# Attention block with a causal convolution: output products of ten groups of four blocks as seven products instead of eight

## The chip, the cores and the metric

The kernel runs on one core of a Trainium2 chip. The metric is the device time of one execution in microseconds (us). Before the change it is 2947.87 us, the median of 3 runs (2943.88 to 2949.68).

## The reference

Four sequences of 1024 tokens with 1024 features, f32 throughout. A conditioned attention layer is added to x, and then a causal convolution over tokens with four taps (the taps are the rows of `cond`):

```
scale, shift = split(emb @ W_emb + b_emb)
xn = rms_norm(x, g_norm) * (1 + scale) + shift
q, k, v = split(xn @ W_qkv)                  # 16 heads of 64
q, k = rms_norm(q, g_q), rms_norm(k, g_k)
attn = softmax(q @ k.T / 8)
o = attn @ v
x = x + (o + o @ W_out)                      # o @ (W_out + I)
x = x + causal_conv1d(x, cond) + b           # K = 4, per feature
```

## The kernel before

Work goes by *units*: one sequence b, one pair of heads c, one half of the queries. There are 64, 16 for each sequence. A unit takes the scores of its two heads against the keys in eight steps (`Unit.scores`, matrix products in line 626, copied out of PSUM in line 634), the running maximum on VectorE (643), the maximum over partitions on GpSimd (648), the shift on VectorE (662), exp on ScalarE (666), the sum on GpSimd (668), and in the next unit the product with v (689) and the sum over keys (709). `divide` (749) writes o of the pair, transposed, and it is stored in DRAM (`scrO`).

Between these steps lie *pieces* of other work, which `between(p)` lists for unit p in seven slots. A projection piece (586) is one of seven products of the qkv projection of a later pair of pairs: that projection already works with seven products for eight, on sums of its inputs (`Chunk.combine`, `scrA`) and of its weights (`Weights.combine`, `scrB`). An output piece (`Out`) takes one block of 128 features by 512 tokens of one sequence: transposes of x into PSUM (805), eight matrix products with a column block of W_out, into whose diagonal block the identity was added (799, 819), a copy to SBUF (837), the last tap on ScalarE (839), three taps on VectorE (851), transposes (862), and the store. From unit 16 on each unit has one output of the sequence before (`plan`); in the last 16 units the numbers are 1, 0, 1, 0, 1, 0, 1, 1, 0, 1, 0, 1, 3, 3, 3, 0 (`last_plan`). The outputs of the last sequence follow at the end. o comes back from DRAM in `gather`, one tile of 256 KB for each block of features in eight buffers (tag `ob`). Weight blocks use the same buffers in the first units.

The order on TensorE, VectorE, ScalarE and GpSimd is the order in which the Python program emits instructions. A planned clock (`tick`, `clock`) decides when deferred steps are emitted: `defer` after a time, `defer_quiet` not while the shifts and exps run (`loud`), `defer_gap` in the time in which VectorE would wait for the maximum over partitions (`fill_gap`, once in a unit), and `need` at once. `split` puts the last 25 us of a unit's pieces (`BEHIND`) behind its last scores, beside the softmax. All transfers are issued on SP, which works through them in an order of the scheduler's own; a transfer that waits holds those behind it.

## Time and profile before

| what | value |
|---|---|
| median of 3 runs | 2947.87 us |
| the profiled execution, its span | 2953.38 us, 2951.6 us |
| TensorE, VectorE, ScalarE, GpSimd busy | 96%, 75%, 57%, 48% |
| granted TensorE clock, mean | 0.988 |
| bytes moved, mean rate | 411.89 MB, 140 GB/s |

The profile is one execution. A matrix product in f32 appears as two records. A group's busy time is the union of its instructions, its mean is that of one. "Idle before" is the time for which the engine stood still ahead of the group's instructions, with what ended it.

### The profile page before, as it was taken

To read this page: it belongs to the slowest core of one execution; us is meant where nothing else is said; L and a number is where in the kernel's file an instruction comes from. 1 tells how busy PE (TensorE), PEld (TensorE's weight loads), DVE (VectorE), ACT (ScalarE), POOL (GpSimd) and SP (SyncE) were. 2 spreads that over 40 slices of the span, in tenths; PEclk is the share of its full clock that TensorE was granted. 3 is DMA by queue.
4 is the path that set the end of the run, shared out by engine and by line. 5 is a ranking of instruction groups with operands and counts; after the bars stand their busy time and mean duration, and the time that the engine had idled before them with its cause. 6 is when DMAs were issued, how large, how long until landed. Compare 5 with 4: busy or idle time off the path is not lost.

```text
span 2951.6 us, 32110 instructions
## 1 busy us (share of the span) xinstructions
PE 2830.6 (96%) x10601; PEld 1336.0 (45%) x10601; DVE 2228.2 (75%) x2563; ACT 1694.3 (57%) x2233; POOL 1402.3 (48%) x574
## 2 busy tenths in 40 slices
PE   7989988999999999999999999999999999999898
PEld 3544434444444444444444444444444444444344
DVE  3578878888877777787877777878777877787863
ACT  3155757765656666665555666665565656565432
POOL 2045555556645544545544553545555555553420
PEclk9999999999999999999999999999999999999999
DMA  7764445643333454543533354553343333323333
GB/s 275 254 214 149 148 162 165 197 132 111 115 111 112 146 168 156 177 132 104 157 118 93 126 164 150 177 159 107 100 154 109 103 115 100 111 79 111 108 96 114
DMA packets 401085, 411.89 MB, mean 140 GB/s; under 512 B 40544, under 2 KB 331672, under 8 KB 400920
## 3 DMA queue, kind: packets, MB, share of 16 engines
q1 hardware_dynamic: 400920, 409.84, 43.9%
q8 instruction: 85, 1.39, 0.2%
q14 instruction: 80, 0.66, 0.1%
HBM read 334.26 MB, written 75.48 MB: 139 GB/s over the span
## 4 chain that ended last, share of the span: by engine, by line
PE 75%; DVE 9%; ACT 7%; POOL 3%; issue 2%; DMA 2%; SPq 1%; DVEq 0%; ACTq 0%; POOLq 0%
PE pqkv_P L586 29%; PE po L819 14%; PE pav L689 14%; PE s L626 13%; ACT sp L634 3%; DVE mx L643 2%; POOL sum L668 2%; DVE sp L662 2%; ACT sp L666 2%; DVE y L851 1%; POOL mb L648 1%; PE tot L709 1%; PE qkt L457 1%; PE otp L862 1%; PE po L805 1%
## 5 line engine op out<-in xcount | busy, mean ns | idle before, releaser
L586 PE MATMUL pqkv_P<-w_P,a 128*128 128x384 f32 x3504 | 1189.9, 492 | 27.5 <-issue 11.3
L668 POOL TENSOR_TENSOR sum<-sum,sp 128x1024 f32<-128x1024 f32 x384 | 974.9, 2539 | 58.9 <-ACT sp L666 32.4
L586 PEld LDWEIGHTS pqkv_P<-w_P,a 128*128 128x128 f32 x3504 | 650.7, 191 | 493.2 <-issue 73.2
L634 ACT COPY sp<-s 128x1024 f32<-128x1024 f32 x512 | 511.1, 1015 | 461.7 <-PE s L626 363.9
L643 DVE TENSOR_TENSOR mx<-mx,sp 128x1024 f32<-128x1024 f32 x384 | 524.5, 1366 | 223.0 <-ACT sp L634 199.1
L662 DVE TENSOR_TENSOR sp<-sp,mbp 128x1024 f32<-128x1024 f32 x512 | 604.6, 1212 | 34.3 <-ACT mbp L657 34.2
L648 POOL PARTITION_ALL_REDUCE mb<-mx x64 | 223.9, 3499 | 837.6 <-DVE mx L643 513.5
L666 ACT ACTIVATE sp<-sp 128x1024 f32<-128x1024 f32 x512 | 526.6, 1055 | 117.1 <-DVE sp L662 113.3
L626 PE MATMUL s<-qT,kT 64*128 64x512 f32 x2048 | 520.3, 624 | 40.6 <-ACT sp L634 24.9
L689 PE MATMUL pav<-sp,v 128*64 128x512 f32 x2048 | 472.5, 604 | 0.0
L819 PE MATMUL po<-ob,wo 128*128 128x512 f32 x992 | 441.0, 597 | 2.5 <-DMA ob<-scrO 1.6
L851 DVE SCALAR_TENSOR_TENSOR y<-x,cols,y 128x512 f32<-128x512 f32 x192 | 324.2, 1689 | 109.0 <-ACT y L839 104.4
L668 POOL TENSOR_TENSOR sum<-sp,sp 128x1024 f32<-128x1024 f32 x64 | 151.3, 2363 | 476.3 <-ACT sp L666 293.1
L626 PEld LDWEIGHTS s<-qT,kT 64*128 64x128 f32 x2048 | 171.3, 186 | 333.4 <-issue 167.8
L689 PEld LDWEIGHTS pav<-sp,v 128*64 128x64 f32 x2048 | 136.8, 138 | 321.8 <-issue 309.9
L819 PEld LDWEIGHTS po<-ob,wo 128*128 128x128 f32 x992 | 184.6, 192 | 212.9 <-issue 204.1
L643 DVE TENSOR_TENSOR mx<-sp,sp 128x1024 f32<-128x1024 f32 x64 | 126.9, 1983 | 86.3 <-ACT sp L634 85.5
L837 ACT COPY x<-po 128x512 f32<-128x512 f32 x64 | 37.5, 586 | 228.3 <-PE po L819 211.9
L605 DVE TENSOR_TENSOR qk<-u,pqkv_P 128x256 f32<-128x256 f32 x256 | 105.5, 412 | 60.7 <-PE pqkv_P L586 58.7
L657 ACT COPY mbp<-mb 128x1024 f32<-128x1024 f32 x64 | 65.1, 1017 | 123.7 <-POOL mb L648 123.6
L449 DVE TENSOR_TENSOR qk<-qk,ms 128x1024 f32<-128x1024 f32 x64 | 123.0, 1922 | 2.2
L435 ACT ACTIVATE sq<-qk 128x512 f32<-128x512 f32 x128 | 76.0, 626 | 55.4 <-DVE qk L605 55.4
(84 smaller groups left out, 1659.5 us busy)
## 6 DMA issues: line engine op xcount, KB each, us to landing
a<-scrA SPq DMA_DIRECT2D x215, 512.0 KB
w_P<-scrB SPq DMA_DIRECT2D x64, 768.0 KB
w_P<-in_L_cond_W_qkv_dram SPq DMA_DIRECT2D x144, 256.0 KB
wo<-in_L_cond_W_out_dram SPq DMA_DIRECT2D x128, 256.0 KB
scrA<-r SPq DMA_DIRECT2D x26, 896.0 KB
xc<-in_x_dram SPq DMA_DIRECT2D x64, 256.0 KB
out_dram<-ot SPq DMA_DIRECT2D x64, 256.0 KB
rec<-scrR SPq DMA_DIRECT2D x124, 128.0 KB
```

What stands on the lines that cost most here:

```text
L449: nc.vector.tensor_mul(qk, qk, self.ms[g].unsqueeze(2).to_broadcast([P, 4 * HT, D]))
L586: nc.tensor.matmul(pm, (chunks[0, k].r(place) if a is None else a[:, k, :])[:, t % 2 * P : (t % 2 + 1) * P], w[:, k, :], start=(k == 0), s ...
L626: nc.tensor.matmul(ps[:, h, :], pr.kT[kt // HT][h * D : (h + 1) * D, kt % HT * P : (kt % HT + 1) * P], pr.qT[self.half][h * D : (h + 1) * ...
L634: nc.scalar.copy(sp, ps)
L643: nc.vector.tensor_max(self.mx, self.mx if kt > 1 else self.sp[0], self.sp[kt])
L648: nc.gpsimd.partition_all_reduce(self.mb.rearrange("p h q -> p (h q)"), self.mx.rearrange("p h q -> p (h q)"), P, bass_isa.ReduceOp.max,)
L662: nc.vector.tensor_sub(self.sp[kt], self.sp[kt], self.mb)
L666: nc.scalar.activation(sp, sp, AF.Exp)
L668: nc.gpsimd.tensor_tensor(self.sum, self.sum if kt > 1 else self.sp[0], sp, ALU.add)
L689: nc.tensor.matmul(self.pav[h * D : (h + 1) * D, :], self.pr.v[kt // HT][:, kt % HT, h * D : (h + 1) * D], self.sp[kt][:, h, :], start=(kt ...
L819: nc.tensor.matmul(self.pm, self.w[kh][:, k % KH, :], oTs[b, k, half], start=False, stop=(k == NJ - 1),)
L851: nc.vector.scalar_tensor_tensor(self.y, self.x1[:, k : k + HN], cols[:, r : r + 1], self.y, ALU.mult, ALU.add)
```

## The change

For sequences 0 and 1 and for half of the outputs of sequence 2, four outputs (features j and j + 4, both halves of the tokens) are made together in a `Quad`, of seven products with four matrix products each. The input is halves of o and four sums of them (`OutSums`, made once for each sequence and stored in `scrS`), the weight quarters of W_out + I and four differences of them (`OutWeights`, made in units 8 to 14 and stored in `scrW`). A sum of products is kept in two SBUF tiles (`u2`, `u4`) and added on VectorE. The products start in unit 18, seven in four units, later seven in five. The other eight outputs of sequence 2 are whole products in units 60 to 62, and those of sequence 3 follow as before. Tiles of tag `ob` are now two of 1 MB instead of eight of 256 KB, for weights, sums and o; input tiles of the projection (tag `a`) are three instead of four. The diagonal add moves from GpSimd to VectorE for the remaining whole outputs, and the halo copy from VectorE to ScalarE. `x1` has two buffers, the taps of sequence 2 are always deferred out of the loud time, which ends 4 us later, and outputs are stored once they are 30 us old. The sum over keys of the last two units takes four products of 32 rows each instead of two of 64.

```diff
-        for e in list(idle):
+        for e in sorted(idle, key=lambda e: e[2][2][0] != "qk"):
...
             d, k = self.d, self.k
             self.b = {}
+            four = apool.tile([P, 4, HN], F32, tag="ob", name=f"b_{self.name}", bufs=2)
             for kh in range(2):
                 for y in range(2):
-                    t = apool.tile([P, HN], F32, tag="ob", name=f"b_{self.name}_{kh}_{y}", bufs=8)
+                    t = four[:, 2 * kh + y, :]
                     self.b[kh, y] = t[:, :W3]
...
-            return apool.tile([P, KH, QN], F32, tag="a", name=name, bufs=4)
+            return apool.tile([P, KH, QN], F32, tag="a", name=name, bufs=3)
...
-            loud[1] = loud[0] + NT * step + 1.0
+            loud[1] = loud[0] + NT * step + LOUD
...
-            oT = apool.tile([P, HN], F32, tag="oT", name=f"oT_{self.name}", bufs=3)
+            oT = apool.tile([P, HN], F32, tag="oT", name=f"oT_{self.name}", bufs=2)
...
+            nc.sync.dma_start(scrO[b][self.half][:, c, :], oT)
+    scrO = [
+        [dram.tile([P, NJ, HN], F32, tag=f"o_{b}_{h}", name=f"scrO_{b}_{h}") for h in range(2)] for b in range(B)
+    ]
     def gather(b, half):
-        for k in range(NJ):
-            if (b, k) == (B - 1, NJ - 1):
-                continue
-            need("oT", b, k, half)
-            if (b, half) == (B - 1, 1):
-                if k % 2 == 0:
-                    pair = apool.tile([P, KH, QN], F32, tag="a", name=f"ob_{b}_{k}_{half}", bufs=4)
-                    pair = pair.rearrange("p k t -> p (k t)")
-                ob = pair[:, k % 2 * HN : (k % 2 + 1) * HN]
+        for kh in range(2):
+            n = KH - kh if b == B - 1 else KH
+            for k in range(n):
+                need("oT", b, kh * KH + k, half)
+            if half and b == B - 1:
+                four = apool.tile([P, 8, QN], F32, tag="r", name=f"ob_{b}_{kh}_{half}", bufs=2)
+                four = four.rearrange("p i t -> p (i t)").rearrange("p (k t) -> p k t", t=HN)
             else:
-                ob = apool.tile([P, HN], F32, tag="ob", name=f"ob_{b}_{k}_{half}", bufs=8)
-            nc.sync.dma_start(ob, scrO[b, k, half])
-            oTs[b, k, half] = ob
+                four = apool.tile([P, KH, HN], F32, tag="ob", name=f"ob_{b}_{kh}_{half}", bufs=2)
+            nc.sync.dma_start(four[:, :n, :], scrO[b][half][:, kh * KH : kh * KH + n, :])
+            for k in range(n):
+                oTs[b, kh * KH + k, half] = four[:, k, :]
+    OUT = ("P1", "P2", "P6", "P5", "P3", "P7", "P4")
+    scrW = dram.tile([P, 7, KH, HN], F32, tag="W", name="scrW")
+    OUT_W = {"P5": 0, "P7": 1, "P4": 2, "P6": 3, "P1": 4, "P2": 5, "P3": 6}
+    scrS = [dram.tile([P, 4, KH, HN], F32, tag=f"S_{b}", name=f"scrS_{b}") for b in range(B - 1)]
+    OUT_S = {"P6": 0, "P3": 1, "P7": 2, "P5": 3}
+    class OutWeights:
+        def __init__(self, k):
+            self.k = k
+        def load(self):
+            k = self.k
+            self.b = apool.tile([P, 4, HN], F32, tag="ob", name=f"W_{k}", bufs=2)
+            for kh in range(2):
+                src = w_out[(kh * KH + k) * P : (kh * KH + k + 1) * P, :]
+                nc.sync.dma_start(self.b[:, 2 * kh : 2 * kh + 2, :], src.rearrange("p (y d) -> p y d", y=2))
+            defer_gap(5.0, ("W", k), 0.6, self.diagonals)
+        def diagonals(self):
+            k = self.k
+            for i in (0, 3):
+                d = self.b[:, i, k * P : (k + 1) * P]
+                nc.vector.tensor_tensor(d, d, ident, ALU.add)
+            for i, name in ((0, "P1"), (2, "P2"), (3, "P3")):
+                nc.sync.dma_start(scrW[:, OUT_W[name], k, :], self.b[:, i, :])
+            defer_gap(5.0, ("W", k), 2.8, self.combine)
+        def combine(self):
+            b11, b12, b21, b22 = (self.b[:, i, :] for i in range(4))
+            for dst, p0, p1 in ((b11, b12, b11), (b12, b22, b12), (b22, b22, b11), (b21, b21, b22)):
+                nc.vector.tensor_tensor(dst, p0, p1, ALU.subtract)
+            nc.sync.dma_start(scrW[:, :4, self.k, :], self.b)
+    class OutSums:
+        def __init__(self, b, k):
+            self.b, self.k = b, k
+        def load(self):
+            b, k = self.b, self.k
+            self.o = apool.tile([P, 4, HN], F32, tag="ob", name=f"S_{b}_{k}", bufs=2)
+            for h in range(2):
+                for kh in range(2):
+                    need("oT", b, kh * KH + k, h)
+                    nc.sync.dma_start(self.o[:, 2 * h + kh, :], scrO[b][h][:, kh * KH + k, :])
+            defer_gap(5.0, ("S", b, k), 2.8, self.combine)
+        def combine(self):
+            o11, o12, o21, o22 = (self.o[:, i, :] for i in range(4))
+            for dst, p0, p1, op in (
+                (o22, o21, o22, ALU.add),
+                (o21, o11, o21, ALU.subtract),
+                (o11, o22, o11, ALU.subtract),
+                (o12, o12, o11, ALU.subtract),
+            ):
+                nc.vector.tensor_tensor(dst, p0, p1, op)
+            nc.sync.dma_start(scrS[self.b][:, :, self.k, :], self.o)
+    class Quad:
+        def __init__(self, b, j):
+            self.b, self.j = b, j
+            self.outs = {
+                name: Out(b, c, half) for name, c, half in (("P2", j, 0), ("P3", j + KH, 0), ("P7", j + KH, 1), ("P4", j, 1))
+            }
+            self.o, self.w = {}, {}
+        def load(self, name):
+            b, j = self.b, self.j
+            if name in self.outs:
+                self.outs[name].load_x()
+            o = self.o[name] = apool.tile([P, KH, HN], F32, tag="ob", name=f"o_{b}_{j}_{name}", bufs=2)
+            if name in OUT_S:
+                for k in range(KH):
+                    need("S", b, k)
+                src = scrS[b][:, OUT_S[name], :, :]
+            else:
+                half, kh = {"P1": (0, 0), "P2": (0, 1), "P4": (1, 1)}[name]
+                for k in range(kh * KH, (kh + 1) * KH):
+                    need("oT", b, k, half)
+                src = scrO[b][half][:, kh * KH : (kh + 1) * KH, :]
+            nc.sync.dma_start(o, src)
+            for k in range(KH):
+                need("W", k)
+            w = self.w[name] = wpool.tile([P, KH, P], F32, tag="wo", name=f"wq_{b}_{j}_{name}", bufs=3)
+            nc.sync.dma_start(w, scrW[:, OUT_W[name], :, j * P : (j + 1) * P])
+        def product(self, name):
+            b, j = self.b, self.j
+            out = self.outs.get(name)
+            if name == "P7":
+                out.residual(whole=True)
+                nc.vector.tensor_add(self.u4, self.u4, out.pm)
+            if name in ("P2", "P3", "P4"):
+                out.residual()
+                pm = out.pm
+            else:
+                pm = ps_m.tile([P, 512], F32, tag="m", name=f"po_{b}_{j}_{name}")
+            for k in range(KH):
+                nc.tensor.matmul(
+                    pm,
+                    self.w[name][:, k, :],
+                    self.o[name][:, k, :],
+                    start=(k == 0 and name not in ("P2", "P3", "P4")),
+                    stop=(k == KH - 1),
+                )
+            tick(3.5)
+            if name == "P1":
+                self.u2 = apool.tile([P, HN], F32, tag="ou2", name=f"ou2_{b}_{j}", bufs=1)
+                nc.scalar.copy(self.u2, pm)
+            elif name == "P5":
+                self.u4 = apool.tile([P, HN], F32, tag="ou4", name=f"ou4_{b}_{j}", bufs=1)
+                nc.vector.tensor_add(self.u4, self.u2, pm)
+            elif out:
+                out.open()
+                nc.vector.tensor_add(out.x1[:, PAD:], self.u4 if name in ("P3", "P7") else self.u2, pm)
+                out.last_tap(out.x1[:, PAD:])
+            if name in ("P6", "P7"):
+                nc.vector.tensor_add(self.u2, self.u2, pm)
...
-            defer(4.5 if j < KH or b >= B - 2 else 8.0, ("wo", self.name), self.diagonal)
+            defer(4.5, ("wo", self.name), self.diagonal)
         def diagonal(self):
             d = self.w[self.j // KH][:, self.j % KH, :]
-            (nc.vector if self.b == B - 1 or self.b == B - 2 and self.half else nc.gpsimd).tensor_tensor(d, d, ident, ALU.add)
-        def residual(self):
+            nc.vector.tensor_tensor(d, d, ident, ALU.add)
+        def residual(self, whole=False):
...
-            if taken:
-                need("y", taken.pop())
+            self.open()
+            nc.scalar.copy(self.x1[:, PAD:], self.pm)
+            self.last_tap(self.pm)
+        def open(self):
+            if len(taken) == 2:
+                need("y", taken.pop(0))
             taken.append(self.name)
-            x1 = apool.tile([P, PAD + HN], F32, tag="x1", name=f"x1_{self.name}", bufs=1)
-            self.x1 = x1
-            if half:
-                nc.vector.tensor_copy(x1[:, :PAD], halo[:, j, :])
-            else:
-                nc.vector.memset(x1[:, :PAD], 0.0)
-            nc.scalar.copy(x1[:, PAD:], self.pm)
+            x1 = self.x1 = apool.tile([P, PAD + HN], F32, tag="x1", name=f"x1_{self.name}", bufs=2)
+            nc.scalar.copy(x1[:, :PAD], halo[:, self.j, :] if self.half else none)
+        def last_tap(self, src):
+            j = self.j
             self.y = apool.tile([P, HN], F32, tag="x", name=f"y_{self.name}", bufs=6)
             nc.scalar.activation(
                 self.y,
-                self.pm,
+                src,
                 AF.Identity,
                 bias=cols[:, R_CB + j : R_CB + j + 1],
                 scale=tap_self[:, j : j + 1],
             )
-            (defer if self.b >= B - 2 and self.half else defer_quiet)(2.0, ("y", self.name), self.taps)
+            (defer if self.b == B - 1 else defer_quiet)(2.0, ("y", self.name), self.taps)
...
-    BEHIND = 25
+    BEHIND = 26
...
+    AGE = 30.0
+    LOUD = 5.0
+    AGE_REST = 5.0
+    W_AT = 3
+    outs, norms, chunks, weights, doubles, quads = {}, {}, {}, {}, {}, {}
+    LAST = (B - 1) * 2 * NJ
+            if n in (PB - 1, PB) and i % 14 == W_AT:
+                free(lambda: OutWeights((n - PB + 1) * 2 + i // 14).load())
+    def out_next(m):
+        at = REST.index(m) + 1 if m in REST else 0
+        out_load(m + 1 if m not in REST else REST[at] if at < len(REST) else LAST)
...
-    plan = [1] * NB
-    last_plan = [1, 0, 1, 0, 1, 0, 1, 1, 0, 1, 0, 1, 3, 3, 3, 0]
-    assert sum(plan) == NB and sum(last_plan) == NB and len(plan) == NB
+    NQ = 2 * KH + KH // 2
+    NG = NQ * len(OUT)
+    def products_until(p):
+        q = p - NB - 2
+        return min(max(q * 7 // 4 if q < 2 * NB else 56 + (q - 2 * NB) * 7 // 5, 0), NG)
+    REST = [(B - 2) * NB + h * NJ + j for h in range(2) for j in (2, 3, 6, 7)]
+    REST_PLAN = {p: n for p, n in zip(range(B * NB - 4, B * NB - 1), (3, 3, 2))}
+    def out_load_product(g):
+        b, i = divmod(g, 4 * len(OUT))
+        j, i = divmod(i, len(OUT))
+        if g < NG:
+            if i == 0:
+                quads[b, j] = Quad(b, j)
+            quads[b, j].load(OUT[i])
+    def out_product(g):
+        b, i = divmod(g, 4 * len(OUT))
+        j, i = divmod(i, len(OUT))
+        def step():
+            if g == 0:
+                out_load_product(0)
+            quad = quads[b, j]
+            quad.product(OUT[i])
+            if OUT[i] in quad.outs:
+                late.append((clock[0], quad.outs[OUT[i]].store))
+            out_load_product(g + 1)
+        pieces = [(3.95 if OUT[i] in ("P2", "P3", "P7", "P4") else 3.5, step)]
+        return [(0.0, lambda: store(AGE))] + pieces
...
-        pl = last_plan if b == B - 1 else plan
-        slots[0].append((0.45, store))
-        ks = range(sum(pl[:i]), sum(pl[: i + 1])) if b else ()
-        if b and i == 0:
-            slots[0] += [(0.0, lambda: gather(b - 1, 0)), (0.0, lambda: out_load((b - 1) * NB))]
-        for a, k in enumerate(ks):
-            m = (b - 1) * NB + k
-            at = 4 if len(ks) == 1 else 2 * a + 1
-            slots[at] += out_pieces(m)
-            if a:
-                slots[at].append((0.45, store))
-            if k == NJ - 1:
-                slots[at].append((0.0, lambda: gather(b - 1, 1)))
-            slots[at].append((0.0, lambda m=m: late.append(outs[m].store)))
+        slots[0].append((0.0, lambda: store(AGE)))
+        d, k = divmod(p - 11, NB)
+        if 0 <= d < B - 1 and k % 2 == 0 and k < NJ:
+            slots[0].append((0.0, lambda: OutSums(d, k // 2).load()))
+        for a, g in enumerate(range(products_until(p), products_until(p + 1))):
+            slots[(2, 5)[a]] += out_product(g)
+        if p in REST_PLAN:
+            at = sum(n for q, n in REST_PLAN.items() if q < p)
+            for m in REST[at : at + REST_PLAN[p]]:
+                if m in REST[:: len(REST) // 2]:
+                    slots[6].append((0.0, lambda m=m: gather(B - 2, m // NJ % 2)))
+                slots[6] += [(0.0, lambda: store(AGE_REST))] + out_pieces(m)
+                slots[6].append((0.0, lambda m=m: late.append((clock[0], outs[m].store))))
```

## The prediction

> **What bounds the kernel now.** I read the page's engine table and groups first, then TensorE's timeline for one unit, then the stretches by stage, and the chain last.
>
> ```profile
> PE 2830.6 (96%) x10601; PEld 1336.0 (45%) x10601; DVE 2228.2 (75%) x2563; ACT 1694.3 (57%) x2233; POOL 1402.3 (48%) x574
> ...
> L819 PE MATMUL po<-ob,wo 128*128 128x512 f32 x992 | 441.0, 597 | 2.5 <-DMA ob<-scrO 1.6
> ```
>
> TensorE is busy 96% of the span, but modelled ends make that figure soft. The timeline of one unit of the second batch is harder evidence:
>
> ```profile
> 1009.76 7.03 PE L819 MATMUL po<-ob,wo 128*128 128x512 f32 x16
> 1016.63 5.32 PE L586 MATMUL pqkv_P<-w_P,a 128*128 128x384 f32 x16
> 1021.88 1.99 PE L626 MATMUL s<-qT,kT 64*128 64x512 f32 x8
> ...
> 1029.62 2.04 PE L626 MATMUL s<-qT,kT 64*128 64x512 f32 x8 [0.25 <-ACT sp L634]
> 1031.60 3.65 PE L689 MATMUL pav<-sp,v 128*64 128x512 f32 x16
> ```
>
> Each row starts where the last ends; the only wait is 0.25 us. So in this stage what TensorE has to do is the time. The chain shows what removing such work is worth. It lists every whole output product as one piece:
>
> ```profile
> 1009.92 6.87 PE po L819 x16
> ...
> 1052.15 6.88 PE po L819 x16
> ...
> 2196.49 6.87 PE po L819 x16
> ...
> 2275.13 6.87 PE po L819 x16
> ...
> 2354.06 6.87 PE po L819 x16
> ...
> 2432.70 6.87 PE po L819 x16
> ```
>
> One output's 8 matrix products (16 records, two passes each for f32) take 6.87 us, so 0.859 us per product. With an output in each unit the units are 42.2 to 42.7 us apart. At the end of the table the plan has an output in every second unit: 78.64, 78.93, 78.64 us for two units, against 2 x 42.67 = 85.3. Leaving out one output gave back 6.6 us. Its TensorE work is 6.87 plus 0.44 (residual transposes) plus 0.59 (output transposes) = 7.9. So 84% of removed TensorE time comes back; the rest turns into small waits.
>
> The other engines' room, by stretches (us, then busy PE, PEld, DVE, ACT, POOL, clock, DMA share, GB/s):
>
> ```profile
> 165.00:783.00 618.00, 574.95 (x2226) 267.37 (x2225) 505.90 (x579) 400.00 (x516) 342.13 (x128) 0.98 0.48 154
> ...
> 1009.00:1051.60 42.60, 42.35 (x159) 19.90 (x158) 31.37 (x32) 23.81 (x34) 22.02 (x10) 1.00 0.41 131
> 1263.00:1306.00 43.00, 42.32 (x168) 19.82 (x166) 38.25 (x45) 29.22 (x37) 22.38 (x9) 1.00 0.47 144
> ```
>
> VectorE is at 74% in a plain unit, 89% in a unit that also prepares the next batch, 82% in the first batch, where TensorE idles 43 of 618 us. VectorE is the engine to watch.
>
> **What it removes.** Ten groups of four outputs go from 4 x 8 = 32 products to 7 x 4 = 28; 24 outputs stay whole. 512 becomes 280 + 192 = 472. 40 x 0.859 = 34.4 us of TensorE time, all in stages where TensorE sets the pace. Residual and output transposes stay as many. Times 0.84 (the ratio above): 28.9 us come back. That ratio includes the smaller cover that every wait has behind a shorter unit.
>
> Moved: outputs begin in unit 18 rather than 16, and the last three full units get 3, 3 and 2 whole outputs rather than 3, 3 and 3. Each matrix product is still done once, where TensorE is the bound at both places, so 0.
>
> **What it adds on VectorE.** Rows of the tiles y and oT (shortest, median, longest in ns), and a group kept apart by shape:
>
> ```profile
> L851 DVE SCALAR_TENSOR_TENSOR y<-x,cols,y x192: 741/1515/2900, 803.7 to 2945.6; 128x512 f32<-128x512 f32 x192
> ...
> L749 DVE TENSOR_TENSOR oT<-pav,rec x64: 676/682/692, 220.5 to 2876.7; 128x512 f32<-128x512 f32 x64
> ...
> L507 DVE TENSOR_TENSOR b<-b,b 128x384 f32<-128x384 f32 x48 | 33.7, 701 | 8.7 <-DMA b<-in_L_cond_W_qkv_dram 7.6
> ```
>
> - A group of seven products has 8 adds with one operand in PSUM (P2, P6, P5, P3, P4 one each, P7 three). The nearest row is L749, 0.68 us, steady. 80 x 0.68 = 54.4. Against it, 32 halo copies (24.7 us in the groups) and 32 memsets (2.0) go over to ScalarE: net +28 us over 42 units, 0.7 per unit.
> - 12 sums of o with 4 adds each, both operands in SBUF: by L507 scaled from 384 to 512 elements 0.93 us, so 3.7 per set, 44.9 in all. Weights: 4 x (4 x 0.93 + 2 x 0.42, the VectorE row of the diagonal add) = 18.2.
> - Here a rule speaks against the change. L851, with two SBUF inputs, takes from 0.74 to 2.9 us; L749, reading PSUM, never over 0.69. The Trainium skill (SBUF — State Buffer, "SBUF: two separate sides") says that a VectorE operation with two SBUF inputs and a GpSimd operation reading SBUF take an exclusive lock on one port pair, so one waits for the whole of the other. By it each of the 64 SBUF adds could wait one GpSimd add (2.54 us): 64 x 2.54 = 163 us of VectorE time more. By the row, which holds such waits already in its mean, 63 in all. I take the row: these adds are released in the gap in which VectorE waits for the maximum over partitions. The 40 diagonal adds that leave GpSimd (0.94 each) help a little.
>
> Sum on VectorE: 28 + 44.9 + 18.2 = +91 us, 2319 of some 2930, 79% against 75%. In a plain unit it lies in 11 us of idle: 0. If that cover went, 1.8 us in each of 42 units, 76 us. In the first batch 33 us of it falls into ten units, with 7 us idle in each: between 0 and 15, I take 2. ScalarE: 30 fewer copies of 0.586 and 64 tiny ones of 0.2: -5 us. It now waits for VectorE's add before it takes the last tap; that wait lies beside TensorE: 0.
>
> **What it adds in waits.** Tiles of o come as 1 MB in two buffers. Product g+1's tile loads from the end of product g-1, normally some 38 us ahead. But a set of sums occupies one of the two from its load to its store. While it does, the next tile can start only when the last product ends, and by the order of instructions three projections stand between (3 x 2.58 + 0.44 = 8.2 us; in the other case 9.1). Eight of the twelve sets fall so. What 1 MB takes is not in the trace. The chain shows smaller loads:
>
> ```profile
> 124.73 6.33 DMA a<-scrA
> ...
> 137.41 5.16 DMA a<-scrA
> ...
> 2674.84 4.89 DMA ob<-scrO
> ```
>
> 256 KB took 4.89 us, 512 KB 5.2 to 6.3; so 0.3 to 1.4 per 256 KB, and 1 MB some 5.8 to 9.1, estimated. The Trainium skill (DMA: Bandwidth & Descriptors, "Anatomy of one DMA — SWDGE (gpsimd) path") fits 2.0 us plus bytes by 436 GB/s, which would be 4.4 us and no wait; it is for another queue than SP's, and already the 256 KB row exceeds it. By the rows the wait is 0 to 1.5, plus what holds SP up; 0.5 x 8 = 4 us, bounds 0 and 24.
>
> - Projection inputs have three buffers, not four. SP then waits for the pair of projections just before, and has two pairs (10.3 us) for a load of 5 to 6. Queued behind on SP: the small transfers of the row sums and the next w and o. 215 loads; TensorE waited for one, 0.4 us. I take 0, bounds 0 and 20.
> - SP issues 84 more transfers, some 0.4 us each, 34 us over the whole span. Bytes: +70 (o) +24 (sums) +11 (W) -8 -20 +17.5 = +95 MB on 412, so 140 GB/s becomes 175; the first 50 us ran at 306. 0.
> - Whole outputs at the end gather 1 MB at a change of half where 256 KB pieces could follow each other: 2.5 us late, in a unit of 46 us with 7 idle. 0, bounds -6 (the unit with two outputs) and 5.
> - Start: weight tiles are freed four at a time. SP's loads begin up to 2.7 us later (the next stores are at 54 to 58, not 53). 1 us, bounds -2 and 6.
>
> **Sum.** -28.9 + 2 + 4 + 1 = -21.9. Against its own execution: span 2951.6 (2953.4 with what lies around) to 2929.7 (2931.5). That execution is 5.5 above the median of the runs, 2947.9; from the median, **2926**.
>
> **Rivals.**
> - *VectorE becomes the bound in part* (0.22). For: 89% in preparing units, 82% in the first batch, and adds that may wait for GpSimd. Against: the gap before the shifts. In full it costs 1 us in each of 8 preparing units, 15 in the first batch where I took 2, and 1 us for each pinned tile where I took 0.5: 8 + 13 + 4 = 25 more, which would leave no gain. At half of that, 12.5: **2938**.
> - *Slower* (0.10): SP's queue comes late. With three buffers each load of projection inputs waits at SP's head for a TensorE event one pair later, and what stands behind comes late in turn. For: SP already waits there 103 us in 66 cases. Against: TensorE waited 0.4 us. Price: 215 loads, one in four 1 us late is 54; with 21.9 off, **2980**. It decides from 22 us, 0.1 us per load.
> - *Nothing changes* (0.06): the waits equal the gain: **2948**.
> - *The ratio is 1, not 0.84, and no load is late* (part of the likeliest): -34.4, **2913**.
>
> **How the numbers follow.** The forecast holds with 0.62, range 2912 to 2933. VectorE 0.22, nothing 0.06, slower 0.10. About 0.2% (6 us) is what a measurement can tell. Faster 0.84 (the first two), within 0.06, slower 0.10. The range runs from 2909 (ratio 1 and 4 us from the shorter last unit) to 2950, past the second rival and the third, leaving most of the slower one out.
>
> **What would show it.** Right: output products 472, some 3.44 us per group of four; units with two of them 42 us apart, with one 38; no PE wait for o over 2 us. VectorE near 2320 us. Wrong: PE idle before the output or projection products on DMA (pinned tile, three buffers); PE waiting for ScalarE's score copies (VectorE late); a first batch longer than 618 us by over 5; a GpSimd idle time before the maximum that grows.

## The result and the profile after

On one chip, against the kernel before, the change gives 2915.59 us (median of 6 runs, 2911.43 to 2922.92) against 2945.89 (6 runs, 2943.3 to 2949.68). The ratio is 0.9899, with an interval of 0.9882 to 0.9915: faster by 1.0%. The forecast was 2926 with 2909 to 2950. The profiled spans are 2951.6 before and 2917.7 after, so 33.9 us went (30.3 by the medians) where the sum had 21.9. That is close to the 34.4 us of the products, but not by the way the sum describes: several of its small terms are wrong in size or sign, others are missing, and they nearly cancel.

The engine line of the page after, and the groups that answer to those shown of before (busy us, mean ns of one, idle before):

```profile
PE 2797.4 (96%) x10529; PEld 1322.4 (45%) x10529; DVE 2183.2 (75%) x2652; ACT 1692.7 (58%) x2269; POOL 1347.7 (46%) x534
...
L986 DVE SCALAR_TENSOR_TENSOR y<-x,cols,y 128x512 f32<-128x512 f32 x192 | 249.4, 1303 | 61.2 <-ACT y L974 56.6
...
L950 PE MATMUL po<-ob,wo 128*128 128x512 f32 x352 | 159.6, 606 | 4.4 <-DMA ob<-scrO 4.4
L881 PE MATMUL po_P<-o_P,wq_P 128*128 128x512 f32 x320 | 144.0, 592 | 0.2 <-DVE u L610 0.2
...
L881 PE MATMUL po<-o_P,wq_P 128*128 128x512 f32 x240 | 108.0, 592 | 0.0
```

The output products are now 352 + 320 + 240 records here and 32 in the last block's own group (from the tile `oT`): 944, two each, so 472 as counted. The seven products (L881) waited for no transfer at all. VectorE's busy time did not rise by 91 us, it fell by 45. The three taps (L986) alone fell by 75; their group of before was:

```profile
L851 DVE SCALAR_TENSOR_TENSOR y<-x,cols,y 128x512 f32<-128x512 f32 x192 | 324.2, 1689 | 109.0 <-ACT y L839 104.4
```

TensorE's timeline of one unit with two products:

```profile
1252.91 3.60 PE L881 MATMUL po<-o_P,wq_P 128*128 128x512 f32 x8
1256.35 5.32 PE L589 MATMUL pqkv_P<-w_P,a 128*128 128x384 f32 x16
...
1264.53 3.60 PE L881 MATMUL po_P<-o_P,wq_P 128*128 128x512 f32 x8
...
1278.87 2.04 PE L629 MATMUL s<-qT,kT 64*128 64x512 f32 x8 [0.31 <-ACT sp L637]
```

As before, the rows follow each other and the one wait is 0.31 us. The chain has the product as a piece of 3.43 to 3.44 us, half of the 6.87 of a whole output:

```profile
1253.08 3.44 PE po L881 x8
...
1264.69 3.43 PE po_P L881 x8
```

The same stretches of time as before, which hold almost the same units (us, then busy PE, PEld, DVE, ACT, POOL, clock, DMA share, GB/s):

```profile
165.00:783.00 618.00, 576.75 (x2219) 266.84 (x2220) 511.14 (x602) 399.26 (x512) 339.38 (x129) 0.98 0.53 171
1009.00:1051.60 42.60, 42.35 (x168) 19.33 (x166) 32.57 (x40) 24.94 (x35) 19.63 (x9) 1.00 0.54 180
1263.00:1306.00 43.00, 42.69 (x163) 20.24 (x162) 34.55 (x39) 26.79 (x34) 20.67 (x8) 1.00 0.54 174
```

TensorE fills a unit as before. What VectorE lost and gained shows in its groups, kept apart by shape:

```profile
L747 DVE TENSOR_TENSOR oT<-pav,rec 128x512 f32<-128x512 f32 x64 | 44.0, 688 | 42.5 <-DMA rec<-scrR 39.5 <-issue 2.9
...
L835 DVE TENSOR_TENSOR S<-S 128x512 f32<-128x512 f32 x48 | 33.0, 688 | 1.2
...
L809 DVE TENSOR_TENSOR W<-W 128x512 f32<-128x512 f32 x16 | 14.0, 875 | 0.4
...
L900 DVE TENSOR_TENSOR ou<-ou,po_P 128x512 f32<-128x512 f32 x20 | 13.7, 684 | 13.9 <-PE po_P L881 13.9
```

One row is new in kind: ahead of `oT`, the product with the reciprocal of the row sums, VectorE now stands idle 39.5 us for the transfer of the reciprocals, in 18 waits. Before it was 4.9 us in 4:

```profile
DVE oT L749 <- DMA rec<-scrR: 4.9, 4, 2.0
```

Only 7.3 us of these waits lie between units 8 and 16, where they will turn out to cost time (experiment 4).

**Where the 33.9 us went.** A mark that both traces have is the start of each unit's sum over keys on TensorE (L709 before, L707 after). The mark of unit u, counted from 0, lies in unit u + 1; "units 8 to 16" is the time from mark 8 to mark 16, and "units 1 to 8" that from the first mark to mark 8. The table takes the difference of the times between two marks, beside the difference in TensorE work between them, from the records there: a product at 0.859 us, the transposes of a residual at 0.44 and of an output at 0.59.

| stretch between marks | before, us | after, us | difference | TensorE work | rest |
|---|---|---|---|---|---|
| to the first mark | 200.4 | 193.5 | -6.9 | 0 | -6.9 |
| units 1 to 8 | 316.4 | 307.7 | -8.6 | 0 | -8.6 |
| units 8 to 16 | 304.5 | 315.4 | +10.9 | -7.3 | +18.2 |
| units 16 to 48 | 1401.0 | 1361.5 | -39.5 | -37.0 | -2.5 |
| units 48 to 59 | 439.2 | 450.3 | +11.0 | +17.3 | -6.2 |
| units 59 to 63 | 210.8 | 210.3 | -0.5 | -7.3 | +6.8 |
| to the end | 79.3 | 79.0 | -0.3 | 0 | -0.3 |
| all | 2951.6 | 2917.7 | -33.9 | -34.4 | +0.5 |

Rounding leaves 0.1 here and there. The "rest" is not nothing everywhere: it is two gains ahead of unit 8, a loss of 18.2 in units 8 to 16, small gains in the middle and a loss in the tail. A second profile of the changed kernel (span 2916.8) has its marks within 1.6 us of the first from unit 16 on, but 4.1 us earlier at unit 8; so the split between the second and the third row is good to some 4 us, their sum to 1. Early gains also shrink again: the five kernels without the products (the kernel before and experiments 6 to 9) reach mark 8 between 508.8 and 516.7 us, but mark 16 between 818.0 and 822.1. So part of the 18.2 can be the loss of what was gained ahead of it.

### The profile page after: what moved, and what is told of

It is laid out like the page before. It is cut to its first block, busy times and chain, and to the rows that moved or that the text cites. A ratio compares the mean times of both kernels' runs of the same rounds, so it can differ in the third digit from the quotient of the medians.

```text
span 2917.7 us, 32188 instructions
## 1 busy us (share of the span) xinstructions
PE 2797.4 (96%) x10529; PEld 1322.4 (45%) x10529; DVE 2183.2 (75%) x2652; ACT 1692.7 (58%) x2269; POOL 1347.7 (46%) x534
## 3 DMA queue, kind: packets, MB, share of 16 engines
q8 instruction: 84, 1.38, 0.2%
## 4 chain that ended last, share of the span: by engine, by line
PE 71%; DVE 13%; ACT 7%; DMA 4%; issue 3%; POOL 1%; SPq 1%; DVEq 0%; ACTq 0%; POOLq 0%
PE pqkv_P L589 28%; PE pav L692 14%; PE s L629 13%; PE po L950 5%; DVE mx L646 4%; PE po_P L881 4%; PE po L881 3%; ACT sp L637 3%; DVE sp L665 2%; ACT sp L669 1%; PE qkt L459 1%; DVE y L986 1%; PE tot L707 1%; DMA rec<-scrR 1%; PE otp L997 1%
## 5 line engine op out<-in xcount | busy, mean ns | idle before, releaser
L671 POOL TENSOR_TENSOR sum<-sum,sp 128x1024 f32<-128x1024 f32 x384 | 958.1, 2495 | 73.2 <-ACT sp L669 43.1
L646 DVE TENSOR_TENSOR mx<-mx,sp 128x1024 f32<-128x1024 f32 x384 | 514.6, 1340 | 166.2 <-ACT sp L637 137.8
L986 DVE SCALAR_TENSOR_TENSOR y<-x,cols,y 128x512 f32<-128x512 f32 x192 | 249.4, 1303 | 61.2 <-ACT y L974 56.6
L646 DVE TENSOR_TENSOR mx<-sp,sp 128x1024 f32<-128x1024 f32 x64 | 107.8, 1685 | 103.7 <-ACT sp L637 103.7
L950 PE MATMUL po<-ob,wo 128*128 128x512 f32 x352 | 159.6, 606 | 4.4 <-DMA ob<-scrO 4.4
L881 PE MATMUL po_P<-o_P,wq_P 128*128 128x512 f32 x320 | 144.0, 592 | 0.2 <-DVE u L610 0.2
L881 PE MATMUL po<-o_P,wq_P 128*128 128x512 f32 x240 | 108.0, 592 | 0.0
```

What stands on the lines that cost most here:

```text
L646: nc.vector.tensor_max(self.mx, self.mx if kt > 1 else self.sp[0], self.sp[kt])
L671: nc.gpsimd.tensor_tensor(self.sum, self.sum if kt > 1 else self.sp[0], sp, ALU.add)
L881: nc.tensor.matmul(pm, self.w[name][:, k, :], self.o[name][:, k, :], start=(k == 0 and name not in ("P2", "P3", "P4")), stop=(k == KH - 1),)
L950: nc.tensor.matmul(self.pm, self.w[kh][:, k % KH, :], oTs[b, k, half], start=False, stop=(k == NJ - 1),)
L986: nc.vector.scalar_tensor_tensor(self.y, self.x1[:, k : k + HN], cols[:, r : r + 1], self.y, ALU.mult, ALU.add)
```

## The experiments

Each was timed beside the kernel before on the same chip. Diffs are against the changed kernel unless another is named.

**1. The eighth product back** (P1 made twice in one accumulation).

```diff
-            for k in range(KH):
+            times = 2 if name == "P1" else 1
+            for a in range(times):
+                for k in range(KH):
...
-                    start=(k == 0 and name not in ("P2", "P3", "P4")),
-                    stop=(k == KH - 1),
+                        start=(a == 0 and k == 0 and name not in ("P2", "P3", "P4")),
+                        stop=(a == times - 1 and k == KH - 1),
```

> The changed kernel, in which the product P1 of each of the ten groups is accumulated twice (so its outputs are not the reference's): 40 matrix products more, no other work, no other data. It prices the TensorE time that the change takes away. Theory: in these units TensorE's own work is the time, and 3.44 us per group come back in full: +34 us against the changed kernel, so level with the kernel before or up to 4 us above. The step of the prediction (0.84 of it comes back): +29. Rival: the gain comes from something else (shorter waits, cheaper taps), and the products lie partly beside waits: +15 or less.

2948.0 us (13 runs), ratio 0.9987 (0.9979 to 0.9996), span 2948.1. The marks move away from the changed kernel's by 3.2 us per group, from +2.8 at unit 16 to +34.8 at unit 58: 32.0 of 34.4, so 93% in this profile, where the forecast had 84%. Each of the ten groups costs 2.6 to 3.4 us in the one unit that its product lies in. The whole is less sure: the spans of the two profiles differ by 30.4 us, since the tail of this one is some 4 us shorter, and the timed ratios by 0.0088, 26 us, with an interval of some 6 either way. So the units' lengths speak for 93%; the timed runs do not tell it from 84%. All the rest of the change together is worth little: with 32 products' time per group again, the kernel is 0.13% from the one before.

**2. The sums of o and the differences of the weights left out** (loads, stores and transfers stay).

```diff
-            for dst, p0, p1 in ((b11, b12, b11), (b12, b22, b12), (b22, b22, b11), (b21, b21, b22)):
-                nc.vector.tensor_tensor(dst, p0, p1, ALU.subtract)
...
-                nc.vector.tensor_tensor(dst, p0, p1, op)
```

> The changed kernel without the 64 adds on VectorE that make the sums of o and the differences of the weights (loads and stores stay, the outputs are not the reference's). Some 47 us of VectorE time go. Theory: what units 8 to 16 lose (19 us like for like) comes from the late transfers of the row sums, of which these adds hold up a part, since the reciprocal stands behind them on VectorE: -5 us. Rival, VectorE is the bound in the first batch: -15 or more. Rival, SP's queue alone: 0 within 3.

2903.3 us (4 runs), ratio 0.9838 (0.9824 to 0.9851), span 2899.1, so 18.6 less than the changed kernel. That is the size of the rival, VectorE as the bound, and not of the theory; experiments 4 and 5 decide on the cause. The two groups are busy 47 us in all, but the time does not come back where most of them stand: the marks part by 12.7 us between units 8 and 16, by 1.5 up to 20, and by 0.5 from there to 58, although 8 of the 12 sets of sums lie there. So some 30 of these adds (16 of weights, 12 to 16 of o) cost 13 us in the first batch, while the later ones are nearly free. And without them VectorE's wait for the reciprocals falls to a third, between units 8 and 16 from 7.3 us to nothing, although every transfer is still there:

```profile
DVE oT L747 <- DMA rec<-scrR: 13.3, 9, 2.7
```

**3. The loud time as before** (taps may stand beside the shifts and exps again).

```diff
-    LOUD = 5.0
+    LOUD = 1.0
```

> The changed kernel with LOUD back at 1.0, so that the taps on VectorE are deferred 4 us less and run again beside the sums on GpSimd. Theory: the taps become dearer (mean 1.30 us back toward 1.69, VectorE +60 us or more), but VectorE is not the bound, so the time is within 5 us of the changed kernel. Rival, cheaper taps are a part of the gain: +10 us or more.

2924.43 us (4 runs), ratio 0.9908 (0.9895 to 0.9922), span 2923.3. The group of the taps:

```profile
L986 DVE SCALAR_TENSOR_TENSOR y<-x,cols,y 128x512 f32<-128x512 f32 x192 | 300.4, 1569 | 65.7 <-ACT y L974 61.2
```

1569 ns against 1303: the same work at another place takes 51 us more of VectorE. Its price in time is small, +5.6 us in this profile, which it has at unit 48 and keeps to the end; by the ratios 0.0009, which is inside the intervals. VectorE's busy time and the kernel's time are two things.

**4. The division 3 us later on the planned clock.** The row sums go to DRAM, come back as a small tile, are inverted on VectorE, go out and come back as `rec`; then VectorE multiplies.

```diff
-    DIVIDE = 18.0
+    DIVIDE = 21.0
```

> The changed kernel with DIVIDE 21 in place of 18: the division of o is emitted 3 us later on VectorE. Theory: VectorE stands 39.5 us in 18 waits for the transfer of the reciprocals, with shifts behind it that free the PSUM of the scores; 3 us later most of these waits are gone (under 12 us), and the time falls by 4 to 10 us, most of it in units 8 to 17. Rival, these waits lie beside other work: 0 within 3. Rival, the PSUM of the value product comes free too late: +5 or more.

2904.81 us (5 runs), ratio 0.9842 (0.9828 to 0.9855), span 2903.9, 13.8 less (17 by the ratios); expected were 4 to 10. VectorE's waits for `rec` are all but gone:

```profile
DVE oT L747 <- DMA rec<-scrR: 3.0, 3, 1.7
```

Between units 8 and 16 it is 306.7 us long instead of 315.4, near the 302.7 of the kernel without the adds. The granted clock of this stretch says the same. Two rows, the changed kernel and this one:

```profile
501.19:816.63 315.44, 292.98 (x1135) 135.43 (x1133) 258.79 (x314) 197.63 (x247) 169.03 (x64) 0.98 0.53 173
```

```profile
502.86:809.54 306.68, 287.82 (x1135) 134.64 (x1133) 261.77 (x313) 197.26 (x247) 171.89 (x64) 1.00 0.55 180
```

The same 1135 records take 5.2 us less of TensorE, at a clock of 1.00 instead of 0.98, and the waits in TensorE's timeline are 3.5 us less (18.7 against 22.2). VectorE is no less busy: the loss was not its load but its standing still. The place agrees. In the changed kernel, VectorE waits for `rec` at 644.6, 719.6 and 799.0 us (3.0, 2.2 and 2.1 us); the three units between marks in which these lie are 2.9, 3.9 and 2.9 us longer than in this kernel, 9.7 together.

What happens is to be seen at the second of these in the changed kernel, first on VectorE, then on SP, then in the chain:

```profile
703.99 2.85 DVE L835 TENSOR_TENSOR S<-S 128x512 f32<-128x512 f32 x4
706.77 0.55 DVE L604 TENSOR_TENSOR u<-u,pqkv_P 128x384 f32<-128x384 f32 x1
707.23 0.20 DVE L733 RECIPROCAL few<-few 128x8 f32<-128x8 f32 x1
...
719.58 0.69 DVE L747 TENSOR_TENSOR oT<-pav,rec 128x512 f32<-128x512 f32 x1 [2.16 <-DMA rec<-scrR]
720.18 1.21 DVE L665 TENSOR_TENSOR sp<-sp,mbp 128x1024 f32<-128x1024 f32 x1
```

```profile
700.69 0.34 SPq L730 DMA_DIRECT2D few<-scrT  x1
...
706.88 0.57 SPq L836 DMA_DIRECT2D scrS<-S  x1
707.49 0.63 SPq L566 DMA_DIRECT2D a<-scrA  x1
708.17 1.03 SPq L735 DMA_DIRECT2D scrR<-few  x1
```

```profile
708.17 5.41 DMA scrR<-few
713.58 0.02 issue
713.59 0.46 SPq L738
...
714.10 5.45 DMA rec<-scrR
```

The small tile was asked for at 700.69. But the four sums of o (2.85 us) stand ahead of its reciprocal on VectorE. The store of the reciprocals is issued behind the 1 MB store of the sums and takes 5.41 us; `rec` is asked for as soon as it has landed. So `oT` finds no `rec` at its turn, VectorE stands 2.16 us, and the shift behind it, which frees a PSUM buffer of the scores, comes late; TensorE's scores then wait 2.83 us for it. The adds can thus act in two ways, by their own time and by putting the store of the sums next to that of the reciprocals. In the changed kernel, all eight stores of reciprocals issued within 3 us after a store of sums whose landing the trace tells took 4.1 to 6.0 us, the other 32 a median of 2.4. No run parts the two.

**5. The adds left out and the later division together.** Parts 2 and 4 in one.

> The sums of o and the differences of the weights are left out (so the output is not the reference's), and the division by the row sums comes 3 us later on the planned clock. Alone, leaving the adds out gave some 18 us and the later division some 17 by the timed ratios (15 and 14 by the spans). One cause (the adds cost time because they make the row sums' round trip through DRAM late, and VectorE waits for it): taken together they give hardly more than one alone, ratio 0.982 to 0.984, span 2897 to 2903. Two causes (the adds cost VectorE's own time, the round trip is late by itself): the gains add up, ratio 0.978 to 0.979, span near 2888.

2900.39 us (4 runs), ratio 0.9835 (0.9819 to 0.985), span 2896.3. Mostly one cause, then: each alone gives 18.6 and 13.8 by the spans, both 21.4, not 32. Units 8 to 16 take 304.7 us here and 306.7 in experiment 4: once the division comes later, the adds cost 2.0 us there, not 12.7. From the first mark to unit 16, where the split at unit 8 plays no part, it is 5.3 instead of 13.8. Over the whole they still cost 7.6 us by the spans, but 0.0007 by the ratios, inside the intervals.

**6. The later division in the kernel before** (diff against the kernel before: the same line).

> The kernel before with the division 3 us later on the planned clock. Theory (the late round trip of the row sums comes with the change; before, VectorE waited only 4.9 us for it): 0.998 to 1.001, at most 4 us less. Rival (the later division is worth its 14 to 17 us to any version): 0.994 to 0.996.

2952.17 us (14 runs), ratio 1.0007 (0.9998 to 1.0015). The later division is worth nothing where no `rec` is late: the disturbance came with the change.

**7. Projection inputs in three buffers** (against the kernel before; the last gather, which used the same tag, takes another).

```diff
-            return apool.tile([P, KH, QN], F32, tag="a", name=name, bufs=4)
+            return apool.tile([P, KH, QN], F32, tag="a", name=name, bufs=3)
```

> The kernel before with three buffers for the projection's inputs in place of four (the last gather uses the tiles r, as in the changed kernel). The prediction's step, and the theory: 0 within 4, no TensorE wait for a over 1 us. The slower rival of the prediction: +22 us or more, with TensorE waiting for a.

2954.06 us (22 runs), ratio 1.0008 (1.0001 to 1.0016), span 2952.6. TensorE has no wait for `a` among its waits for transfers. If there is a price, it is some 2 us. The slower rival, at 54 us, would have been seen here as far as it rests on the three buffers; the 84 further transfers on SP are not in this kernel.

**8. Tiles of 1 MB alone** (against the kernel before: weights in the first units, o, one DRAM tensor for each half, the last gather in another tag).

```diff
+            four = apool.tile([P, 4, HN], F32, tag="ob", name=f"b_{self.name}", bufs=2)
...
-                    t = apool.tile([P, HN], F32, tag="ob", name=f"b_{self.name}_{kh}_{y}", bufs=8)
+                    t = four[:, 2 * kh + y, :]
...
-                ob = apool.tile([P, HN], F32, tag="ob", name=f"ob_{b}_{k}_{half}", bufs=8)
+                four = apool.tile([P, KH, HN], F32, tag="ob", name=f"ob_{b}_{kh}_{half}", bufs=2)
```

> The kernel before with one part of the change alone: weight tiles, r tiles and gathered o as two tiles of 1 MB, and o of a half in one tensor in DRAM; the outputs stay whole products. Theory: the 7 us that the changed kernel gains up to its first unit and the 9 that it gains in units 1 to 8 come from this (fewer transfers that wait for one another on SP): -7 to -15 us at unit 8, and -5 to -12 in all, a part being lost at the last change of half (+4). The prediction's step (later loads at the start): +1. Rival, the gain has another source: 0 within 3.

2947.59 us (22 runs), ratio 0.999 (0.9983 to 0.9997). At the first mark it is 8.1 us ahead of the kernel before, as the changed kernel is (6.9). But the profile of the kernel before is a late one here: the three kernels of experiments 6, 7 and 9, which have no 1 MB tiles, reach that mark at 195.6 to 197.2 us instead of 200.4, and the ten with them at 191.5 to 193.9. So the gain at the start goes with these tiles, and is some 2 to 9 us, 5 between the means. In units 1 to 8 it gains nothing more (-7.9 at unit 8), and it loses 4.7 in units 8 to 16 and 1.7 after, down to -1.5 at the end.

**9. The normalization first in the gap** (against the kernel before). In units 6 and 7 the kernel before takes 46.0 and 44.5 us, the changed kernel 39.8 and 39.9. One line of the change acts there on VectorE's order alone.

```diff
-        for e in list(idle):
+        for e in sorted(idle, key=lambda e: e[2][2][0] != "qk"):
```

> The kernel before with one line of the change alone: in the gap before the shifts the normalization of q and k goes first, ahead of the sums of the qkv weights. TensorE's order stays the same; on VectorE only these blocks change places. Theory (this line, which the prediction did not cost, is what makes units 6 and 7 of the first batch 39.8 and 39.9 us long in the changed kernel against 46.0 and 44.5): units 6 and 7 together 8 to 11 us shorter, the whole 0.996 to 0.998. Rival (the gain of units 1 to 8 comes from other work that lies ahead of it): units 6 and 7 stay at 90 us, ratio 0.999 to 1.001.

2951.21 us (13 runs), ratio 1.0002 (0.9994 to 1.0011). Units 6 and 7 take 46.6 and 44.6 us. This theory fell. What makes the 8.6 us of units 1 to 8 stays open: alone it is not the order in the gap, not the tiles, not the three buffers (45.9 and 44.7 in experiment 7), not the later division before (47.6 and 44.3). Every kernel with the seven products has it, also without their adds (experiment 2: 39.1 and 39.9). The traces hold a lead. From the first mark on, VectorE makes 0, 8, 4, 4, 0, 8 and 8 sums of qkv weights (`b`) in units 1 to 7 in every kernel without the products, and 4, 4, 4, 4, 4, 4 and 8 in every kernel with them. That order comes from the planned clock: the change plans 0 instead of 0.45 us for `store` at the head of each unit, and the kernel before, emitted with that one number at 0, has these sums in every unit too. No run times it alone, so whether it is worth the 8.6 us is not shown.

**10. The products from unit 16 on**, as the outputs before the change.

```diff
-        q = p - NB - 2
-        return min(max(q * 7 // 4 if q < 2 * NB else 56 + (q - 2 * NB) * 7 // 5, 0), NG)
+        q = p - NB
+        return min(max(q * 7 // 4 if q < 2 * NB else 56 + (q - 2 * NB) * 7 // 6, 0), NG)
```

> The output products begin in unit 16 instead of 18, still seven in four units, and seven in six at the end. Theory (TensorE sets the pace in both places, so moved products are worth nothing; the small things in units 16 and 17 get the later half of the weight differences sooner): within 4 us of the changed kernel, ratio 0.988 to 0.991. Rival (VectorE is the bound in the first batch and its rest in units 16 and 17 was what caught up): 5 us or more slower than the changed kernel, ratio 0.992 or more.

2962.28 us (6 runs), ratio 1.0047 (1.0032 to 1.0061): 44 us slower than the changed kernel by the ratios, slower than before. The outcome is on the rival's side, but neither named the mechanism. It is TensorE's wait for the tiles of o, 38.4 us:

```profile
PE po_P L881 <- DMA o_P<-scrS: 21.7, 2, 11.7
...
PE po_P L881 <- DMA o_P<-scrO: 16.7, 1, 16.7
```

The 16.7 us are the pinned tile, which the forecast saw in kind. SP's queue at that place:

```profile
788.11 0.56 SPq L836 DMA_DIRECT2D scrS<-S  x1
788.77 0.58 SPq L735 DMA_DIRECT2D scrR<-few  x1
792.62 0.37 SPq L810 DMA_DIRECT2D scrW<-W  x1
793.04 1.90 SPq L738 DMA_DIRECT2D rec<-scrR  x2
794.98 3.05 SPq L862 DMA_DIRECT2D o_P<-scrO  x2
```

A set of sums and a set of weights hold both buffers of tag `ob`; their stores are issued at 788 and 793, so the first o of a product is asked for at 795 and used at 802, 16.7 us late. The other two waits (10.1 and 11.7 us) are the round trip of a sum itself. The chain of the 10.1:

```profile
855.26 5.24 DMA scrS<-S
860.51 0.02 SPq L862
860.56 5.23 DMA o_P<-scrS
```

The last sums of a sequence are stored and loaded back, 10.5 us, with nothing in between. The 11.7 are the same for the next sequence (5.16 and 6.76 us, from 1554). Two units of delay are what keeps this off the path in the changed kernel.

**11. The changed kernel once more, unchanged.**

> The changed kernel as it is, timed beside the next three on one chip, as their measure: a ratio of 0.990 to the kernel before, within 0.002.

2918.45 us (4 runs), ratio 0.9896 (0.9878 to 0.9914).

**12. A version that beats both.** The later division, and the second half of sequence 2's o gathered into buffers of another tag, which are free at that time. In the changed kernel that gather waits for the last product that reads the half before. The chain there:

```profile
2682.67 3.45 PE po L950 x8
...
2686.14 0.37 SPq L924
...
2686.56 0.50 SPq L735
...
2687.11 7.18 DMA ob<-scrO
...
2694.33 6.23 PE po L950 x7
```

```diff
-            if half and b == B - 1:
+            if half and b >= B - 2:
...
-    DIVIDE = 18.0
+    DIVIDE = 21.0
```

> The changed kernel with DIVIDE 21 and with the second half of sequence 2's o gathered into the tiles r, which are free at the end, in place of the two 1 MB tiles that the half before still holds. Theory: the 4.4 us wait of TensorE for that gather is gone and adds to the 16 us that DIVIDE 21 alone gave: 0.983 of the kernel before, -20 us against the changed kernel, and no TensorE wait for ob over 1 us. Rival: unit 61 waits for VectorE anyway (unit 60 has the same three outputs and is as long), then -16 as with DIVIDE alone.

2898.03 us (4 runs), ratio 0.9822 (0.9805 to 0.9839), span 2897.8: 20 us less than experiment 11 beside it, with intervals that do not meet. Against experiment 4, 6.1 us of span less, and 5.3 of these lie between units 59 and 61, where the 7.18 us transfer was.

## Why the prediction was right, and where it was not

The likeliest case came, some 10 us below its time, and its cause, the products' time on TensorE, is shown (experiment 1). That the total came so near is in part luck: gains that the sum does not have (7 us at the start, 8.6 in units 1 to 8) stand against a loss in the first batch that it put at 2 and a tail that it put at 0. By its steps:

- **What bounds.** Right. TensorE at one small wait per unit, output products 3.44 us each. Units with two products are 42.7 to 43.2 us apart and those with one 39, where the text said 42 and 38.
- **Removed, -28.9.** Right in mechanism. The factor 0.84 was worked out from leaving out a whole output, whose transposes and copies go too; by the units' lengths one of eight products returns 93% (experiment 1), which makes the term -32.0. The timed runs, at 26 +- 6 us, allow both. In the steady stage (four units from unit 30, 31, 32, 33 or 34 on) they take 167.4 to 167.9 us against 171.3 to 171.4 before, so 3.4 to 3.9 where 3.44 was removed.
- **VectorE +91 us, 2319.** Wrong by 136. The adds from PSUM were sized right (0.68 each, 80 of them, 54.8), and the halo's 24.7 are gone. The sums of o took 0.688, not 0.93, and with the weights' adds 50.5 us (33.0, 14.0 and 3.5 for the diagonals), not 63. But the larger part is work whose amount the change leaves alone: the taps fell from 324.2 to 249.4, the maximum from 651.4 to 622.4, the combinations of projection inputs from 89.2 to 67.4. The text took all these as fixed durations. Experiment 3 shows how little the taps' are that: with the loud time set back, they cost 51 us more at the same count. What made the other two fall was not tested.
- **The rule on the shared port.** The Trainium skill's rule (SBUF — State Buffer, "SBUF: two separate sides") would have put up to 2.54 us on each of the 64 adds, 163 us. The row put 63. At 50.5 the row was nearer, and still too high: the sums of o run at the 0.688 of an add that reads PSUM, so they seem to meet hardly any GpSimd work where they stand. The taps, at 739 ns shortest and 2836 longest, would fit such a lock, and experiment 3 shows that their mean goes with their place; that a lock is the reason no run shows.
- **First batch +2 (0 to 15).** Wrong size, and the cause only half right. Units 1 to 16 lost 9.6 us, units 8 to 16 alone 18.2. The adds are worth 12.7 of these (experiment 2), near the upper bound. But the text looked for it in VectorE's time, and experiments 4 and 5 show that most of it is the wait of an in-order engine: the adds and their transfers make the reciprocals late. The text had put the small transfers of the row sums on its list of what is queued behind on SP, and then given it zero.
- **Pinned tiles +4.** Zero in the changed kernel: L881 has no wait for a transfer. The mechanism is real and dear where the products start two units sooner (16.7 us once, experiment 10). A load of 1 MB took 5.2 to 7.2 us in the chains (5.23, 6.76, 6.91, 7.18) where the text estimated 5.8 to 9.1; the 4.4 us that the Trainium skill's fit for GpSimd's queue gives (DMA: Bandwidth & Descriptors, "Anatomy of one DMA — SWDGE (gpsimd) path") is under all of these.
- **Three buffers 0, SP's queue 0.** The first is right within some 2 us (experiment 7); the slower rival falls as it was put. The second holds for the projection's inputs. What did come late on SP was the store of the reciprocals behind that of the sums (experiment 4); how much of the 13 us is the queue's no run shows, but with every transfer kept and the adds gone VectorE waits for no `rec` between units 8 and 16 (experiment 2).
- **Start +1.** Wrong sign: -6.9 in these two profiles, some -5 over all, and it comes with the 1 MB tiles (experiment 8). The text counted what larger tiles free later and nothing that they bring.
- **Tail 0.** The gather at the change of half, "2.5 us late" and hidden, cost TensorE a wait of 4.4 us, and moving it away gave 6 (experiment 12). The cover was not there: 7 us of idle in a unit are not idle behind this product.
- **Not in the text:** -8.6 in units 1 to 8 and some -11 in units 16 to 59 beyond the 32.0 of the products (-2.5 and -6.2 in the table, and the 2.4 by which 34.4 exceeds 32.0). The wider quiet time gives 5 to 6 of the second in experiment 3's profile; the others are open.

The rival "VectorE becomes the bound in part" did happen in units 8 to 16, near the full price that it named there (15; the adds cost 12.7), though as standing still rather than as work. It did not carry into the preparing units or the pinned tiles, so its 2938 was too late.

## What to carry to other kernels

When work is added to an engine that executes in order, ask not only whether the engine has room for it but which small round trip through memory passes that engine and its queue: here some 13 us went because sets of four adds and their store stood ahead of a reciprocal of 0.2 us, and a later due time for the consumer took most of it back. An operation's duration in a profile belongs to its place as well as to its kind; the average of the taps fell by a quarter from one schedule to the next. And where a plan starts late by two units, look for the round trip that it waits for before moving it up.

## What the runs showed of the hardware that was not expected

- The same `y` instruction took 1689, 1569 and 1303 ns on average in three schedules (739 at the shortest), with equal shapes and counts.
- Small waits went together with a lower clock: in units 8 to 16 the same number of TensorE records took 292.98 us at a granted clock of 0.98, and 287.82 us at 1.00 in the kernel whose VectorE did not wait for the reciprocals.
- In the changed kernel's chain, which shows the transfers that mattered, the 4 KB store of the reciprocals took 4.88, 5.41 and 5.73 us, and the 1 MB store of the sums 4.74 us: a transfer 256 times as large took no longer. The small one can be much shorter: where the trace tells its landing it took 1.38 us at the least and a median of 2.4 away from the stores of sums.
